# Third block of an attention and expert kernel: the chunk that two experts share is multiplied by their gates, turned to rows

## The chip, the cores and the metric

One core of a Trainium2 chip runs the whole program in one launch. The metric is the device time of one execution in microseconds; three executions of the kernel before are shown, and one further execution was profiled.

## The reference, cut to what matters

The input is x, 32 images of 128 tokens by 144 channels in f32, with one condition vector per image. Three transformer blocks follow each other, with a learned rotation between the first and the second. The change touches only the second half of the third block, a mixture of four experts:

```python
logits = h @ w_gate                       # 4 experts, the top 2 are kept
gate   = softmax over the kept two        # 0 for the others
for e in range(4):
    hidden = gelu(h @ w1[e] + b1[e])      # 144 -> 576
    y     += gate[:, e] * (hidden @ w2[e] + b2[e])   # 576 -> 144
x = x + g_mlp * y
```

All four experts are computed for every token, and the gate is zero for the two that are not kept.

## The kernel before, in words

The work is done in groups of G = 4 images, 8 groups a block. The order of the instructions is written out by hand: the main loop (L1281) runs over ticks, one image of attention each, and each tick has named gaps ("a", "e", "t", "stats", "b0", "b", "den", "pre1", "c", "y1", "y2", "z", "d" in the third block's order). `put(tick, gap, f, ...)` files a piece of other work under a gap, and `put2` files two halves of it in two gaps. Each engine executes its instructions in the order in which they were recorded, and waits for what they need.

An expert has 576 hidden units: four chunks of 128 and a rest of 64. Two experts make a pair, and the two rests share one chunk, number SHARED = 8 of `hid`, the first expert's in partitions 0 to 63 and the second's in 64 to 127. So a pair has NPC = 9 chunks of hidden units. `hid` is [128 units, 9 chunks, 4 images, 128 tokens].

- `moe1` (L1055) calls `fc1` (L930): three chunks at a time, weights as the stationary side, 4 x 128 tokens as the moving side, then GELU by ScalarE into `hid` (L947).
- `moe2` (L1059) calls `fc2` (L949) for one expert and one image: five products of 128x144 accumulate in one PSUM bank `ps_f`. A chunk of `hid` is the stationary side, w2 the moving side. The fifth product uses the shared chunk. Both experts of a pair multiply the same shared chunk, each with a copy of w2 in which the other's 64 rows are zero, so w2 has 10 chunks for 9 chunks of hidden units. VectorE then does acc = ps_f x gate + acc (L1064), with the gate as one number per token, which is a partition here.
- `moe_bias` (L1041) has GpSimd start `acc` with the four gated biases (L1051, L1053). `moe_out` (L1066) multiplies by g_mlp, adds to x and stores (L1069 to L1071).

For a group with first tick t0, the pair's tick is t0 + 8 or t0 + 10. There `moe1` stands in "stats"/"b0" and "den"/"pre1", and `moe2` of the first (even) expert and image 0 in "d". In the next tick come the third part of `moe1` and the even expert's images 1 to 3 ("b", "c", "d"). The second (odd) expert's images follow in gaps "a", "a", "b", "b" of the tick after that. The attention in the same ticks runs through `scores` (L819: ps_s, ps_w, the reduce nm at L854, the exponentials at L861), `weigh` (L867), `sums` (L885), `divide_T` (L897, transposes at L901), `largest_T` (L805, transpose at L808), `divide` (oT, L906), `largest` (q2, L813) and `project_out` (L922). In the pair's tick there is also other work of later groups: `values` (vaug, L802 and L803) beside the first pair, `qk_chunks` and `qk_masked` (the key masks, L727) beside the second.

PSUM has one bank for `ps_o` and seven that `bank` (L78) hands out; a bank comes free when its last reader is done. Every matrix product in f32 leaves two MATMUL records in the profile, a transpose leaves one.

Of the kernel before, what the change touches and what calls it, by code (L numbers as in the profile page):

```python
# [8 lines left out]
F32 = mybir.dt.float32  # L9
# [3 lines left out]
ALU = mybir.AluOpType  # L13
# [4 lines left out]
B, T, C = 32, 128, 144  # L18
# [4 lines left out]
NFC = 5  # L23


SHARED = 8
NPC = 9
MLP_COLS = NFC * (128 + 128 + C)
PAIR_COLS = NPC * 256 + 2 * NFC * C
D = 64  # L30
E = 4
G = 4
# [33 lines left out]
def tile_kernel(ctx: ExitStack, tc: tile.TileContext, a: dict, out: bass.AP):  # L66
    nc = tc.nc
# [10 lines left out]
    def bank(shape, name):  # L78

        n = 1  # L80
        for s in shape[1:]:
            n *= s
        t = ps_m.tile([128, 512], F32, tag="m", name=name)
        v = t[: shape[0], :n]
        if len(shape) == 3:
            v = v.rearrange("p (a b) -> p a b", b=shape[2])
        elif len(shape) == 4:
            v = v.rearrange("p (a b c) -> p a b c", b=shape[2], c=shape[3])
        return v
# [3 lines left out]
    ident = cst[:, K_ID : K_ID + 128]  # L93
# [16 lines left out]
    hid = const.tile([128, NPC, G, T], F32, name="hid")  # L110
# [49 lines left out]
    def views(t, n1, n2):  # L160

        p = Block()
        p.w1, p.w1R = t[:, : n1 * 128], t[:, n1 * 128 : n1 * 256]
        p.w2 = t[:, n1 * 256 : n1 * 256 + n2 * C].rearrange("p (m c) -> p m c", c=C)
        return p
# [452 lines left out]
    gr = defaultdict(dict)  # L618
# [311 lines left out]
    def fc1(g, p, name, m, to, rest_first):  # L930


        hM, hR = gr[g]["hM_m"], gr[g]["hR_m"]
        pss = [bank([128, G, T], f"ps_h_{name}_{m + i}") for i in range(len(to))]
        cols = [slice(128 * (m + i), 128 * (m + i) + 128) for i in range(len(to))]
        tiles = [rows4((m + i) % 3) for i in range(len(to))]
        yield from both(
            [(ps, p.w1[:, c], hM) for ps, c in zip(pss, cols)],
            [(ps, p.w1R[r, c], hR[r]) for ps, c, r in zip(pss, cols, tiles)],
            rest_first,  # L940
        )

        t = small.tile([128, 1], F32, tag="gelu", name=f"gelu_{name}_{m}", bufs=1)
        nc.scalar.activation(t, half, AF.Gelu_apprx_tanh)
        for ps, i in zip(pss, to):
            n = 64 if g[0] < 2 and i == SHARED else 128
            nc.scalar.activation(hid[:n, i], ps[:n], AF.Gelu_apprx_tanh)  # L947

    def fc2(g, w2, i, first, name):  # L949
        ps = bank([128, C], f"ps_f_{name}")  # L950
        for m in range(NFC):
            at0 = first + m if m < NFC - 1 else SHARED
            nc.tensor.matmul(ps, hid[:, at0, i, :], w2[:, m, :], start=m == 0, stop=m == NFC - 1)  # L953
        return ps
# [100 lines left out]
    def moe1(g, pair, part, rest_first):  # L1055
        to = ((0, 1, 2), (SHARED, 3, 4), (5, 6, 7))[part]
        return fc1(g, PAIRS[pair], f"3_{g[1]}_{pair}", 3 * part, to, rest_first)

    def moe2(g, e, i):  # L1059
        acc = gr[g]["acc"][:, i, :]  # L1060
        w2 = PAIRS[e // 2].w2[:, NFC * (e % 2) : NFC * (e % 2) + NFC, :]
        ps = fc2(g, w2, i, 4 * (e % 2), f"3_{g[1]}_{e}_{i}")
        w = gr[g]["cw"][:, i, e : e + 1]
        nc.vector.scalar_tensor_tensor(acc, ps, w, acc, ALU.mult, ALU.add)  # L1064

    def moe_out(g):  # L1066
        acc, n = gr[g]["acc"], g[1]
# [5 lines left out]
    late = L3 = None  # L1073
    PAIRS = []

    def load_pair(n, t):
        nc.sync.dma_start(t, a[f"L3_{n}_mlp"])
        PAIRS.append(views(t, NPC, 2 * NFC))

    def load_late():  # L1080
        nonlocal late, L3
# [6 lines left out]
        for k in ("wgate", "wgateR"):  # L1088
            setattr(L3, k, load(late, f"L3_{k}", q))
        load_pair(0, late.tile([128, PAIR_COLS], F32, name="pair0"))  # L1090

# [74 lines left out]
    stats = defaultdict(list)  # L1166

    def put(tick, gap, f, *args):
        gaps[tick, gap].append((f, args))

    def put2(tick, gap, to, f, *args):

        halves = []

        def first_half():
            halves.append(f(*args))
            next(halves[0])

        def second_half():
            for _ in halves[0]:  # L1180
                pass

        put(tick, gap, first_half)
        put(tick, to, second_half)

    for layer in range(3):
        ahead = 5 if layer == 0 else 6
        for n in range(NG):
            g = (layer, n)
            t0 = first[layer] + n * G  # L1190
            for i in range(G):
                s = layer * B + n * G + i
                if layer == 1 and i == 0:
                    put(t0 - ahead - 2, "d", rotate_T, n)
                    put(t0 - ahead - 1, "b", rotate_in, n)
                    put(t0 - ahead - 1, "d", rotate, n)
                stats[t0 + i - ahead].append((s, "a"))
                stats[t0 + i + 3].insert(0, (s, "m"))
                if layer < 2:
                    put(t0 + i - ahead + 1, "b", ln_T, s, "a")  # L1200
                else:
                    put(t0 + i - ahead, "d", ln_T, s, "a")
                if layer == 0:
                    put(t0 + i + 4, "a", ln_T, s, "m")
                else:
                    put(t0 + i + 3, "d", ln_T, s, "m")
                if layer == 0:
                    put(t0 + i - 3, "c", qk0_project, s)
                    put(t0 + i - 3, "z", qk0_variance, s)
                    put(t0 + i - 2, "b", qk0_guess, s)  # L1210
                    if s == 0:
                        for gap in "bbc":
                            put(-2, gap, qk0_newton, s, nc.vector)
                    else:
                        put(t0 + i - 2, "b", qk0_newton, s)
                        put(t0 + i - 1, "t", qk0_newton, s)
                        put(t0 + i - 1, "t", qk0_newton, s)
                    put(t0 + i - 1, "b", qk0_divide, s)
                    put(t0 + i - 1, "c", qk0_T, s)
            if layer == 0:  # L1220
                for i in (0, 2):
                    put(t0 + i // 2, "b", lambda g=g, i=i: list(values(g, i, 2)))
            elif layer == 1:
                put2(t0, "stats", "b", values, g, 0, 2, True)
                put2(t0 + 1, "stats", "b", values, g, 2, 2, True)
            else:
                put2(t0, "c", "c", values, g, 0, 2, True)
                put2(t0 + 1, "den", "pre1", values, g, 2, 2)
            if layer:
                put2(t0 - 2, "c", "c", qk_chunks, g)  # L1230
                put(t0 - 2, "z", qk_masked, g)
            if layer == 0:
                put2(t0 + 10, "stats", "b", mlp1, g, 0, (0, 1, 2), True)
                put2(t0 + 11, "d", "d", mlp1, g, 3, (3, SHARED), False)
                for i in range(G):
                    put(t0 + 12 + i // 2, "bd"[i % 2], mlp2, g, i)
            elif layer == 1:
                put2(t0 + 8, "c", "c", mlp1, g, 0, (0, 1, 2), True)
                put2(t0 + 9, "c", "c", mlp1, g, 3, (3, SHARED), True)
                for i in range(G):  # L1240
                    put(t0 + (10, 10, 11, 11)[i], "bdbc"[i], mlp2, g, i)
            else:
                put2(t0 + 7, "den", "pre1", gate_logits, g)
                put(t0 + 8, "e", expert_ranks, g)
                put(t0 + 8, "stats", expert_weights, g)
                for i in range(G):
                    put(t0 + 8 + i // 2, "cdab"[i], moe_bias, g, i)
                for pair in range(2):
                    at_ = t0 + 8 + 2 * pair
                    put2(at_, "stats", "b0", moe1, g, pair, 0, True)  # L1250
                    put2(at_, "den", "pre1", moe1, g, pair, 1, False)
                    put2(at_ + 1, "stats", "b0", moe1, g, pair, 2, True)
                    put(at_, "d", moe2, g, 2 * pair, 0)
                    put(at_ + 1, "b", moe2, g, 2 * pair, 1)
                    put(at_ + 1, "c", moe2, g, 2 * pair, 2)
                    put(at_ + 1, "d", moe2, g, 2 * pair, 3)
                    for i in range(G):
                        put(at_ + 2, "aabb"[i], moe2, g, 2 * pair + 1, i)
                put(t0 + 12, "b", moe_out, g)
# [4 lines left out]

    put(first[1] + B - 10, "c", load_L3)
    put(first[1] + B + 7, "d", lambda: load_pair(1, mlps[:, :PAIR_COLS]))

    def fill(tick, gap):
# [224 lines left out]
```

## Time and profile before

| what | value |
|---|---|
| three executions | 1420.84, 1423.7, 1427.12 us (median 1423.7) |
| the profiled execution | 1412.95 us |
| its span | 1411.1 us, granted clock 0.99 |
| third block's expert products, L953 | 1280 records, 16 x 2 x 4 images x 5 products |
| gated sums, L1064 on VectorE | 128, 46.9 us busy, 367 ns each |
| bias sums, L1051 and L1053 on GpSimd | 128 and 96, 386 to 390 and 488 ns each |
| out store, L1071 | 8 of 288 KB |
| a pair's weights | two loads of 1872 KB by SyncE's queue |

In the page, PE is the matrix engine and PEld its weight loads, DVE is VectorE, ACT is ScalarE, POOL is GpSimd and SP is SyncE. A row names line, engine, operation, what was written from what, the shapes, and the count. Busy time and the mean of one follow, and then the idle time of the engine just before such instructions and what ended it. The chain of waits goes back from the last instruction to whatever released each step. The timeline lists start, duration and instruction, and merges equal neighbours (x10). A matmul's row has its full duration, and the next one may start before it ends.

### The profile page before, as it was taken

What the parts mean: (1) busy time and instruction counts of PE and PEld (TensorE: products, weight loads), DVE (VectorE), ACT (ScalarE), POOL (GpSimd) and SP (SyncE); (2) the same over time, 40 slices, a digit from 0 to 9 for tenths busy, and PEclk for the clock granted to TensorE, in tenths of its full rate; (3) what the DMA queues carried; (4) which work ended last, traced back from release to release, by engine and by line L of the source; (5) the groups of instructions that cost most, each with busy time, mean ns of one, the idle gap of its engine ahead of it and who ended that gap; (6) DMA issues with size and microseconds to landing.
All of it is one profiled execution on the core that took longest, in us unless ns stands there. A gap on an engine that the chain in (4) does not pass through costs nothing.

```text
span 1411.1 us, 36544 instructions
## 1 busy us (share of the span) xinstructions
PE 1333.3 (94%) x14530; PEld 976.5 (69%) x14530; DVE 798.3 (57%) x2652; ACT 819.2 (58%) x1912; POOL 623.4 (44%) x1647
## 2 busy tenths in 40 slices
PE   6989898999989988999999999999999999999998
PEld 4667576686766566677767666777776767677765
DVE  5798888877864256565555555544444444343211
ACT  3657767656756445666666666555555555554431
POOL 5567667654643433343333334425252525151522
PEclk9999999999999999999999999999999999999999
DMA  8200000000003100000100000200000000000000
GB/s 221 57 2 19 19 19 2 19 3 20 19 1 117 34 2 18 10 19 10 42 27 18 10 18 11 73 10 18 9 19 9 19 10 18 10 18 2 18 9 9
DMA packets 21612, 34.78 MB, mean 25 GB/s; under 512 B 2176, under 2 KB 12256, under 8 KB 21184
## 3 DMA queue, kind: packets, MB, share of 16 engines
q1 hardware_dynamic: 20848, 31.82, 7.7%
q8 instruction: 117, 1.92, 0.6%
q10 hardware_dynamic: 592, 0.59, 0.2%
q14 instruction: 55, 0.45, 0.1%
HBM read 29.93 MB, written 2.47 MB: 23 GB/s over the span
## 4 chain that ended last, share of the span: by engine, by line
PE 68%; DVE 4%; ACT 2%; issue 1%; POOL 1%; POOLq 0%; DVEq 0%
PE ps_h L673 17%; PE ps_f L953 16%; PE ps_s L849 6%; PE ps_w L849 6%; PE ps_qk L673 5%; PE ps_o L876 5%; PE ps_pj L927 3%; PE ps_v L673 2%; PE ps_o L889 1%; DVE nm L854 1%; PE ps_o L901 1%; PE ps_g L673 1%; DVE oT L906 1%; PE ps_z L985 1%; PE ps_o L808 0%
## 5 line engine op out<-in xcount | busy, mean ns | idle before, releaser
L861 ACT ACTIVATE pr<-ps_w 128x512 f32<-128x512 f32 x384 | 208.5, 596 | 165.4 <-PE ps_w L849 164.7
L854 DVE TENSOR_REDUCE nm<-ps_s 128x4 f32<-128x512 f32 x384 | 246.8, 684 | 82.3 <-PE ps_w L849 68.9
L849 PE MATMUL ps_w<-q,kT 32*128 32x128 f32 x3072 | 236.4, 284 | 0.9 <-ACT hR_m L663 0.6
L849 PE MATMUL ps_s<-kT,qT 32*128 32x256 f32 x1536 | 234.8, 408 | 0.1
L849 PEld LDWEIGHTS ps_w<-q,kT 32*128 32x128 f32 x3072 | 198.6, 187 | 16.1 <-issue 3.6
L947 ACT ACTIVATE hid<-ps_h 128x512 f32<-128x512 f32 (+1 forms) x224 | 119.2, 590 | 119.1 <-PE ps_h L673 119.1
L953 PE MATMUL ps_f<-mlps,hid 128*128 128x144 f32 x1280 | 181.2, 292 | 0.5 <-ACT hid L947 0.5
L953 PEld LDWEIGHTS ps_f<-mlps,hid 128*128 128x128 f32 x1280 | 165.1, 191 | 18.4 <-issue 11.6
L913 POOL TENSOR_TENSOR x_sb<-x_sb,res_a 128x144 f32<-128x144 f32 x96 | 47.0, 489 | 266.8 <-DVE res_a L916 266.7
L1064 DVE SCALAR_TENSOR_TENSOR acc<-ps_f,cw,acc 128x144 f32<-128x144 f32 x128 | 46.9, 367 | 197.6 <-PE ps_f L953 175.8
L849 PEld LDWEIGHTS ps_s<-kT,qT 32*128 32x128 f32 x1536 | 135.0, 186 | 26.8 <-issue 9.2
L673 PE MATMUL ps_h<-hM_m,mlps 128*128 128x512 f32 x304 | 143.8, 606 | 0.0
L876 PE MATMUL ps_o<-pr,vaug 128*32 128x128 f32 x3072 | 104.8, 277 | 0.4 <-issue 0.4
L876 PEld LDWEIGHTS ps_o<-pr,vaug 128*32 128x32 f32 x3072 | 78.7, 110 | 33.8 <-PE ps_w L849 19.0
L673 PEld LDWEIGHTS ps_h<-hM_m,mlps 128*128 128x128 f32 x304 | 53.4, 190 | 66.2 <-issue 64.7
L906 DVE TENSOR_TENSOR oT<-on,ps_o 128x256 f32<-128x256 f32 x96 | 40.0, 417 | 96.3 <-PE ps_o L808 92.9
L953 PEld LDWEIGHTS ps_f<-pair,hid 128*128 128x128 f32 x640 | 82.3, 190 | 9.6 <-issue 8.4
L953 PE MATMUL ps_f<-pair,hid 128*128 128x144 f32 x640 | 86.8, 287 | 0.2 <-ACT hid L947 0.2
L913 POOL TENSOR_TENSOR x_sb<-x_sb,res_m 128x144 f32<-128x144 f32 x64 | 32.8, 512 | 111.4 <-DVE res_m L916 111.2
L634 POOL TENSOR_SCALAR rs_m_a<-mv_m_a 128x2 f32<-128x2 f32 x81 | 15.5, 191 | 142.9 <-DVE mv_m_a L632 115.5
L663 ACT ACTIVATE hM_m<-ps_hT_m,modM 128x128 f32<-128x128 f32 x96 | 44.1, 460 | 58.4 <-PE ps_hT_m L661 58.2
L861 ACT ACT_TABLE_LOAD x55 | 70.6, 1283 | 8.4 <-PE ps_w L849 7.6
(312 smaller groups left out, 2823.2 us busy)
## 6 DMA issues: line engine op xcount, KB each, us to landing
gates<-gates SPq DMA_DIRECT2D x48, 288.0 KB, 3.6
x_sb<-in_x SPq DMA_DIRECT2D x8, 288.0 KB, 10.2
out_x<-x_sb SPq DMA_DIRECT2D x8, 288.0 KB, 2.4
mlps<-in_L_mlp SPq DMA_DIRECT2D x2, 1000.0 KB, 6.3
wt<-in_W SPq DMA_DIRECT2D x6, 320.0 KB, 8.0
pair<-in_L_mlp SPq DMA_DIRECT2D x1, 1872.0 KB, 10.1
mlps<-in_L_mlp SPq DMA_DIRECT2D x1, 1872.0 KB, 7.6
mlps<-in_L_wmod SPq DMA_DIRECT2D x4, 290.0 KB, 6.3
```

The source lines that it names most:

```text
L663: nc.scalar.activation(gr[g][f"{k}_{kind}"][:, i, :], ps[:, k == "hR", :], AF.Identity, bias=m[:, sh, b : b + 1], scale=m[:, sc, b : b + 1],)
L673: nc.tensor.matmul(ps, x, y, start=k == 0, stop=k == 1)
L849: nc.tensor.matmul(o, x, y, start=True, stop=True)
L854: nc.vector.tensor_reduce(nmv[:, at0 : at0 + 2, ONE : ONE + 2], view.rearrange("p (r t k) -> p r t k", t=2, k=T), AX.X, ALU.max, negate=True,)
L861: nc.scalar.activation(pr[:, 4 * e : 4 * e + 4, :].rearrange("p s q -> p (s q)"), view, AF.Exp, scale=SCALE,)
L876: nc.tensor.matmul(po[rows4(j), t, :], v[:, 4 * j + 2 * t + r, :], prs[j // 2][:, 4 * (j % 2) + 2 * r + t, :], start=r == 0, stop=r == 1,)
L906: nc.vector.tensor_tensor(oT, st[s].pop("on"), po, ALU.mult)
L913: nc.gpsimd.tensor_tensor(x_sb[:, b, :], x_sb[:, b, :], t, ALU.add)
L927: nc.tensor.matmul(ps, oT[:, t, :], w[:, t, :], start=t == 0, stop=t == 1)
L947: nc.scalar.activation(hid[:n, i], ps[:n], AF.Gelu_apprx_tanh)
L953: nc.tensor.matmul(ps, hid[:, at0, i, :], w2[:, m, :], start=m == 0, stop=m == NFC - 1)
L1064: nc.vector.scalar_tensor_tensor(acc, ps, w, acc, ALU.mult, ALU.add)
```

## The change

The shared chunk is multiplied by the gates before it enters the product, so that one product with both experts' real w2 rows gives the two gated contributions at once.

The gates of a token lie in one partition, the tokens of `hid` along the free axis. So the gates are spread over 128 columns by GpSimd, 64 for each expert (`cwx`), turned by four transposes on PE, one an image, into a PSUM bank `ps_cw`, and multiplied into `hid[:, SHARED]` by VectorE. For this `shared_by_gate` is filed in the pair's tick, the copy in "stats" and the rest in "y1", ahead of `largest_T`, `divide` and the even expert's image 0 in "d".

`moe2` does four products for each expert. For the even expert it does a fifth, of the gated shared chunk, into a second half of the same bank, and VectorE adds that half to acc with a second instruction. The odd expert has no fifth product. w2 has 9 chunks a pair in place of 10, with no zero rows; the loads shrink accordingly.

```diff
-PAIR_COLS = NPC * 256 + 2 * NFC * C
+PAIR_COLS = NPC * (256 + C)
...
+    def shared_by_gate(g, pair):
+        cwx = late.tile([128, G, 2, 64], F32, tag="cwx", name=f"cwx_{g[1]}_{pair}", bufs=1)
+        cw = gr[g]["cw"][:, :, 2 * pair : 2 * pair + 2]
+        nc.gpsimd.tensor_copy(cwx, cw.unsqueeze(3).to_broadcast([128, G, 2, 64]))
+        yield
+        ps = bank([128, G, T], f"ps_cw_{g[1]}_{pair}")
+        for i in range(G):
+            nc.tensor.transpose(ps[:, i, :], cwx[:, i, :, :].rearrange("p e c -> p (e c)"), ident)
+        nc.vector.tensor_tensor(hid[:, SHARED], hid[:, SHARED], ps, ALU.mult)
+
     def moe2(g, e, i):
-        acc = gr[g]["acc"][:, i, :]
-        w2 = PAIRS[e // 2].w2[:, NFC * (e % 2) : NFC * (e % 2) + NFC, :]
-        ps = fc2(g, w2, i, 4 * (e % 2), f"3_{g[1]}_{e}_{i}")
+        acc, w2, at0 = gr[g]["acc"][:, i, :], PAIRS[e // 2].w2, 4 * (e % 2)
+        ps = bank([128, 2, C], f"ps_f_3_{g[1]}_{e}_{i}")
+        for m in range(4):
+            nc.tensor.matmul(
+                ps[:, 0, :], hid[:, at0 + m, i, :], w2[:, at0 + m, :], start=m == 0, stop=m == 3
+            )
+        if e % 2 == 0:
+            nc.tensor.matmul(
+                ps[:, 1, :], hid[:, SHARED, i, :], w2[:, SHARED, :], start=True, stop=True
+            )
         w = gr[g]["cw"][:, i, e : e + 1]
-        nc.vector.scalar_tensor_tensor(acc, ps, w, acc, ALU.mult, ALU.add)
+        nc.vector.scalar_tensor_tensor(acc, ps[:, 0, :], w, acc, ALU.mult, ALU.add)
+        if e % 2 == 0:
+            nc.vector.tensor_tensor(acc, acc, ps[:, 1, :], ALU.add)
...
                     put2(at_ + 1, "stats", "b0", moe1, g, pair, 2, True)
+                    put2(at_, "stats", "y1", shared_by_gate, g, pair)
                     put(at_, "d", moe2, g, 2 * pair, 0)
...
-        none = np.zeros((64, C), w1.dtype)
-        w2 = np.vstack([w2[0], none, w2[1][:512], none, w2[1][512:]])
+        w2 = np.vstack([w2[0][:512], w2[1][:512], w2[0][512:], w2[1][512:]])
```

In the changed kernel the copy is at L1064, the transposes at L1068, the multiplication at L1069, the products at L1077 and (the shared chunk) L1081, the gated sum at L1085, the addition at L1087, and `moe_out` at L1092 to L1094.

More of the change, by code (lines that the diff above doesn't have):

```diff
@@ L1077, in load_pair @@
         nc.sync.dma_start(t, a[f"L3_{n}_mlp"])
-        PAIRS.append(views(t, NPC, 2 * NFC))
+        PAIRS.append(views(t, NPC, NPC))
     def load_late():
```

## The prediction

> **What bounds the kernel now.** I read the page first (busy shares and the chain that ended last), then the chain in one stretch of the third block, then each engine in order of time around the edited step, and last the rows that give a duration to each operation. The edit lies in the third block's expert part, from about 902 us to the end. The page's head and its chain:
>
> ```profile
> span 1411.1 us, 36544 instructions
> ...
> PE 1333.3 (94%) x14530; PEld 976.5 (69%) x14530; DVE 798.3 (57%) x2652; ACT 819.2 (58%) x1912; POOL 623.4 (44%) x1647
> ```
> ```profile
> PE 68%; DVE 4%; ACT 2%; issue 1%; POOL 1%; POOLq 0%; DVEq 0%
> ```
>
> The chain is PE's. Over 905 to 1300 us the table by stage has PE busy for 394.0 of 395 us, DVE for 168.4 and POOL for 152.2, at a granted clock of 1.00. Busy PE is not PE at its peak, so the pitch of the products decides. The chain through a step of group 2 (start, length, what):
>
> ```profile
> 1049.49 0.22 PE ps_o L901 x2
> 1049.71 0.11 PE ps_o L808
> 1049.82 1.23 PE ps_f L953 x10
> 1051.05 0.11 PE ps_hT_m L660
> 1051.16 0.11 PE ps_hT_m L661
> ```
>
> No gap is left between pieces. Five expert products leave ten records and take 1.23 us, so one 128x144 product costs 0.245 us. A transpose leaves one record and takes 0.11 us.
>
> **Removed.** For each of 8 groups and 2 pairs, 4 images lose one product (the odd expert's fifth). That is 16 x 4 = 64 products, 64 x 0.245 = 15.7 us of PE. They lie in the unbroken chain, four at a time in gaps "a" and "b" of the tick after next, between other PE work, so they count in full.
>
> **Added on PE.** 16 x 4 = 64 transposes of 128x128. Here a rule speaks against the change. The row:
>
> ```profile
> L901 PE MATMUL ps_o<-cst,rdx x192: 272/273/421, 70.0 to 1330.3; 128*128 128x128 f32 x192
> ```
>
> One transpose lasts 273 ns. The Trainium skill (TensorE: Matmul & The Clock Gate, Part 4: PE-mode transpose) puts a 128x128 transpose in a kernel at about 275 ns, most of it access latency, and adds that its result lies in PSUM and needs a further step. At that price 64 x 0.275 = 17.6 us is more than the 15.7 saved, and the change loses 1.9 us. But 273 ns is a latency: in the chain the next instruction follows 0.11 us later. So PE pays 4 x 0.11 = 0.44 us a pair, 7.0 us for 16. I take the pitch, since four transposes stand together and nothing in front of them is late.
>
> Not all 16 pairs pay. In the last three (group 6's second pair and both of group 7) attention is over, and PE stands at the chunk whose GELU is late:
>
> ```profile
> 1344.86 1.00 PE L953 MATMUL ps_f<-mlps,hid 128*128 128x144 f32 x6
> 1344.96 1.57 ACT L947 ACTIVATE hid<-ps_h 128x512 f32<-128x512 f32 x3 [5.39 <-PE ps_h L673]
> 1346.09 0.76 PE L953 MATMUL ps_f<-mlps,hid 128*128 128x144 f32 x4 [0.23 <-ACT hid L947]
> ```
>
> Six records at 0.1225 are issued by 1345.60 and the seventh starts at 1346.09: a hole of 0.49 us, which takes the 0.44. In group 5's second pair the chain has 1.28 us of nm on DVE ahead of L808, which hides it too. Twelve pairs pay: 12 x 0.44 = 5.3 us. If those covers were gone, 1.8 us more.
>
> **Added on DVE, and the new wait.** The product hid x gates is a TENSOR_TENSOR of 128x512 with one side in PSUM. The same form stands in the exponential's part:
>
> ```profile
> L564 DVE TENSOR_TENSOR hid<-hid,ps_even x2: 678/682/687, 192.8 to 199.5; 128x512 f32<-128x512 f32 x2
> ```
>
> So 16 x 0.68 = 10.9 us, and 64 additions into acc at about 0.31 (the row of L916, 128x144 from PSUM) are 19.6 us: 30.5 us on an engine with over 200 us free. Time on DVE is free; lateness is not. The fifth product of the even expert's image 0 must now wait for DVE, and behind it on PE stand two to four transposes, the projection and the next scores. DVE in that step of group 2:
>
> ```profile
> 1049.72 0.23 DVE L803 COPY vaug<-ps_v 128x72 f32<-128x72 f32 x1
> 1049.86 0.42 DVE L906 TENSOR_TENSOR oT<-on,ps_o 128x256 f32<-128x256 f32 x1
> 1050.20 0.41 DVE L813 TENSOR_TENSOR q<-qT,ps_o 128x256 f32<-128x256 f32 x1
> 1051.16 0.37 DVE L1064 SCALAR_TENSOR_TENSOR acc<-ps_f,cw,acc 128x144 f32<-128x144 f32 x1 [0.55 <-PE ps_hT_m L660]
> ```
>
> With the timeline's starts (L808 at 1049.55, first product at 1049.66), the gate transposes take L808's place at 1049.55. The last starts at 1049.88 and ends at 1050.15. DVE starts 0.04 later (as oT does after L808), is free since 1049.95, and ends at 1050.87; PE can go at 1050.92. PE meanwhile does L808 (1049.99) and four products from 1050.10, and reaches the fifth at 1051.08. The wait is hidden with 0.16 us to spare, or 0.04 if its weight load, about 0.12 ahead, has to wait too. Bounds: 0, or about 0.1 us in the eleven pairs of this kind; I allow 0.2 us in all.
>
> What moves on DVE: oT and q end about 1.0 us later (1051.29 and 1051.63), against the projection at 1051.32 + 0.44 = 1051.76 and the next w scores at 1051.92 + 0.44 = 1052.36. Both are in time. In the second pair's step the key masks follow:
>
> ```profile
> 948.03 1.41 DVE L727 TENSOR_SCALAR kT<-ps_qk,cst 128x512 f32<-128x512 f32 x2 [0.45 <-ACT kT L721]
> ```
>
> There the second mask ends at 949.44 now and a bank of ps_w waits for it (start 949.50). In that step the gates' product runs 947.17 to 947.84, oT and q to 948.5, the masks from 948.43 to 949.84. The bank is ready 0.4 us later, PE arrives 0.44 later: no new stall, no gain. The additions delay the next DVE entries (rd, oT, res_a) by 0.31 us; rd has 0.4 us of idle ahead of it in the plain tick of group 0 (920.70 to 921.10), the others stand behind PE work of over 0.5 us. PSUM takes one more bank a pair: its releaser is a GELU or a reduce that is done before PE gets there in each step I followed.
>
> **Added on POOL.** 16 copies of the gates, 128x512. No row has this form. With one input, 191 ns for 2 elements (L634) and 385 for 144 (L1051) give 0.9 us at 512; with two inputs, 488 for 144 and 1400 for 576 give 1.27. I take 0.9, the nearer kind. POOL in the first pair's step:
>
> ```profile
> 1041.65 0.39 POOL L643 TENSOR_SCALAR xr<-x_sb,rs_m_a 128x64 f32<-128x64 f32 x1
> 1043.77 1.40 POOL L1069 TENSOR_TENSOR acc<-acc,gates 128x576 f32<-128x576 f32 x1 [1.73 <-DVE acc L1064]
> ```
>
> The gates are ready at 1039.75, the copy falls into the 1.73 us hole, and PE asks for it near 1049. Without that hole the first bias sum (ends 1049.85, wanted by DVE at 1051.16) still has 1.3 us. Cost 0. No DMA is added or moved on a queue; a pair's load shrinks from 3744 to 3600 columns, outside the chain.
>
> **Sum.** -15.7 + 5.3 + 0.2 = -10.2 us. The profiled execution took 1412.95 us (span 1411.1), so 1402.8. The median of the shown runs, 1423.7, is 10.8 above that execution, and the three spread over 6.3 us; the saving is taken off the median: 1413.5.
>
> **The rivals.**
> - *The main case* (chance 0.69): the sum holds within about 2 us, 1411.5 to 1416.
> - *DVE is late* (0.19): the slack of 0.16 us is too small and every steady tick loses some 0.4 us at the fifth product or at a bank that the masks or additions release. 12 x 0.4 = 4.8, so -5.4: 1418.3. For it: the slack is one semaphore long, and DVE gains 30 us. Against it: in the last pairs PE resumed 0.05 us after the GELU ended.
> - *The won time is given back* (0.06): PE gets earlier to waits on POOL's bias sums or ACT's exponentials, and the 64 products buy nothing but pay for the transposes: near 0, 1423. Against it: no piece of the chain over 1034 to 1054 is ACT's or POOL's.
> - *Slower* (0.06): the round trip lies bare. If PE stops at the first even product instead of the fifth, each steady pair pays the transposes at latency (0.33 + 0.27 = 0.60), the handoffs (0.09) and DVE (0.68), or 1.4 us, and with transposes unpipelined 1.9. At 1.9: 12 x 1.9 = 22.8 - 15.7 = +7.1, 1430.8. It decides from 15.7 / 12 = 1.31 us of PE a pair. Against it: PE waited for single chunks of hid at 1346.09, not for the whole tile, and in the changed order the wait stands on the fifth product.
>
> Half a per cent, 7.1 us, is about what can be told from no change. The main case is faster by more than that except at its edge: faster 0.69, same 0.25 (the two middle rivals), slower 0.06. The range runs from the sum with the runs' spread, 1409, to the DVE case with it, 1421.
>
> **What would show it.** Expert products fall from 1280 to 1152 records in the third block (1920 to 1792 in all). The L1068 transposes start 0.11 us apart; the product L1069 takes 0.68 us; ps_f at L1081 shows no idle ended by hid L1069; the copy L1064 takes about 0.9 us and L1092 still waits for DVE. From 1345 on the stretch shrinks by over 0.9 us a pair. An idle of over 0.3 us at L1081, or a copy over 3 us, makes the prediction wrong.

## The result and the profile after

Ten runs of the changed kernel have a median of 1406.82 us (1398.87 to 1413.49). Ten runs of the kernel before on the same chip have 1420.7 (1410.26 to 1427.12). The ratio, estimated over all these runs, is 0.9912, with a 95% interval of 0.9884 to 0.9939: 12.5 us less, with an interval from 8.7 to 16.5 (the two medians lie 13.9 us apart). The predicted ratio was 1413.5 / 1423.7 = 0.9928, inside that interval. The predicted level, 1413.5 with a range from 1409 to 1421, is not met.

The profiled execution took 1403.12 us, against a forecast of 1402.8 for it. Its page begins, and its chain adds up, as follows:

```profile
span 1401.4 us, 36513 instructions
...
PE 1329.2 (95%) x14466; PEld 973.3 (69%) x14466; DVE 827.4 (59%) x2732; ACT 820.8 (59%) x1912; POOL 633.2 (45%) x1663
...
PE 68%; DVE 3%; ACT 2%; issue 1%; POOL 1%; POOLq 0%; DVEq 0%
```

PE has 64 records fewer (128 product records gone, 64 transposes come), VectorE is busy for 29.1 us more and GpSimd for 9.8 us more, and the chain is still PE's in the same share. The chain through the same step of group 2 as before (start, length, what):

```profile
1047.29 0.22 PE ps_o L901 x2
1047.51 0.44 PE ps_cw L1068 x4
1047.94 0.11 PE ps_o L808
1048.05 0.98 PE ps_f L1077 x8
1049.04 0.27 PE ps_f L1081 x2
1049.31 0.11 PE ps_hT_m L660
```

The four transposes cost 0.44 us in the chain, as their pitch said (the pitch is the distance from one start to the next). The fifth product costs 0.27 us where a product costs 0.245: at most 0.03 us of waiting. The even expert's five products of image 0 take 1.25 us in each of the first eleven pairs, where the kernel before has 1.23, so this wait is 0.3 us in all. The groups of the new instructions (busy us, mean ns of one, idle time before them and what ended it):

```profile
L1087 DVE TENSOR_TENSOR acc<-acc,ps_f 128x144 f32<-128x144 f32 x64 | 19.4, 304 | 2.2
L1081 PE MATMUL ps_f<-pair,hid 128*128 128x144 f32 x64 | 13.4, 290 | 0.0
L1081 PE MATMUL ps_f<-mlps,hid 128*128 128x144 f32 x64 | 13.3, 289 | 0.0
L1092 POOL TENSOR_TENSOR acc<-acc,gates 128x576 f32<-128x576 f32 x8 | 11.2, 1402 | 32.3 <-DVE acc L1085 32.3
L1069 DVE TENSOR_TENSOR hid<-hid,ps_cw 128x512 f32<-128x512 f32 x16 | 11.0, 688 | 37.4 <-PE ps_o L808 23.4 <-ACT hid L947 11.8 <-PE ps_cw L1068 2.1
L1064 POOL COPY cwx<-cw 128x512 f32<-128x512 f32 x16 | 9.8, 612 | 21.8 <-DVE cw L1038 21.8
L1068 PE MATMUL ps_cw<-cst,cwx 128*128 128x128 f32 x64 | 9.8, 275 | 0.0
```

No idle time at L1081 is put down to VectorE, and the eight final multiplications on GpSimd (L1092) still wait for VectorE, as forecast. VectorE around the same step, and below it the fifth product and its weight load (start, length):

```profile
1048.05 0.69 DVE L1069 TENSOR_TENSOR hid<-hid,ps_cw 128x512 f32<-128x512 f32 x1 [0.32 <-PE ps_o L808]
1048.65 0.41 DVE L906 TENSOR_TENSOR oT<-on,ps_o 128x256 f32<-128x256 f32 x1
1048.99 0.41 DVE L813 TENSOR_TENSOR q<-qT,ps_o 128x256 f32<-128x256 f32 x1
1049.41 0.37 DVE L1085 SCALAR_TENSOR_TENSOR acc<-ps_f,cw,acc 128x144 f32<-128x144 f32 x1
...
1047.34 0.60 PE L1068 MATMUL ps_cw<-cst,cwx 128*128 128x128 f32 x4
1048.79 0.30 PEld L1081 LDWEIGHTS ps_f<-pair,hid 128*128 128x128 f32 x2
1048.87 0.43 PE L1081 MATMUL ps_f<-pair,hid 128*128 128x144 f32 x2
```

The multiplication ends at 1048.74, and in the timeline the fifth product starts at 1048.87. Its weight load starts at 1048.79, 0.05 us behind the end of the multiplication. So the round trip is covered but for those 0.03 us, with nothing left over.

**A measure that the spread of runs doesn't reach.** Two profiles of the changed kernel agree within 0.02 us at every image of the third block, while the two executions differ by 2.1 us (1403.12 and 1405.22). Only where TensorE's clock is halved for a few microseconds does the block take longer. So below, "the third block" is the time from the first product of the projection of image 69 (898.08 us before, 897.73 after; the first transposes of gates come some 13 us later) to the end of the span: 513.04 us before and 503.67 after, a difference of -9.37 us against the -10.2 of the sum.

### The profile page after: what moved, and what is told of

The parts are those of the page before. It is cut to its first block, busy times and chain, and to the rows that moved or that the text cites. A ratio compares the mean times of both kernels' runs of the same rounds, so it can differ in the third digit from the quotient of the medians.

```text
span 1401.4 us, 36513 instructions
## 1 busy us (share of the span) xinstructions
PE 1329.2 (95%) x14466; PEld 973.3 (69%) x14466; DVE 827.4 (59%) x2732; ACT 820.8 (59%) x1912; POOL 633.2 (45%) x1663
## 4 chain that ended last, share of the span: by engine, by line
PE 68%; DVE 3%; ACT 2%; issue 1%; POOL 1%; POOLq 0%; DVEq 0%
PE ps_h L673 18%; PE ps_f L1077 9%; PE ps_s L849 6%; PE ps_w L849 6%; PE ps_qk L673 5%; PE ps_o L876 5%; PE ps_f L953 5%; PE ps_pj L927 3%; PE ps_v L673 2%; PE ps_o L889 1%; PE ps_f L1081 1%; DVE nm L854 1%; PE ps_o L901 1%; PE ps_g L673 1%; DVE oT L906 1%
## 5 line engine op out<-in xcount | busy, mean ns | idle before, releaser
L1085 DVE SCALAR_TENSOR_TENSOR acc<-ps_f,cw,acc 128x144 f32<-128x144 f32 x128 | 46.8, 367 | 156.0 <-PE ps_f L1081 74.9
L953 PE MATMUL ps_f<-mlps,hid 128*128 128x144 f32 x640 | 93.3, 293 | 0.0
L953 PEld LDWEIGHTS ps_f<-mlps,hid 128*128 128x128 f32 x640 | 81.9, 190 | 8.1 <-issue 3.3
L1077 PEld LDWEIGHTS ps_f<-pair,hid 128*128 128x128 f32 x512 | 66.8, 190 | 8.4 <-issue 7.7
## 6 DMA issues: line engine op xcount, KB each, us to landing
x_sb<-in_x SPq DMA_DIRECT2D x8, 288.0 KB, 10.2
```

The source lines that it names most:

```text
L1077: nc.tensor.matmul(ps[:, 0, :], hid[:, at0 + m, i, :], w2[:, at0 + m, :], start=m == 0, stop=m == 3)
L1085: nc.vector.scalar_tensor_tensor(acc, ps[:, 0, :], w, acc, ALU.mult, ALU.add)
```

## The experiments

Theory P is the prediction's: PE's pitch decides, so that 64 products are gained and the transposes paid by pitch. All medians and ratios below stand beside runs of the kernel before on the same chip, whose medians were 1418.7 to 1419.3 us in 38 to 64 runs. A difference in us beside a ratio is worked out from the ratio.

### The changed kernel again

> The changed kernel once more, to separate the size of the saving from the spread of runs. Theory P (PE's issue pitch: 64 products at 0.245 us gained, 12 times four transposes at 0.11 us paid): 10.2 us below the kernel before, ratio 0.9928, in whichever place the runs of this chip lie. Rival S (there is a further saving that the sum left out): 12.5 us or more below again, ratio 0.991 or less. If the spread of runs comes from the half-speed stretches of TensorE's clock, the time of a run goes with its granted clock, about 1 us for every 0.1% of clock.

Measured: 1406.72 us (1401.36 to 1417.24), ratio 0.9923 (0.9899 to 0.9948), or 10.9 us less than 1419.3. The third block is 503.68 us, 0.01 us from the first profile. Over the ten runs of the first measurement the time goes with the granted clock: 1413.5 at 0.976 and 0.977, 1398.9 to 1403.2 in four of the five from 0.989 up (1410.2 in the other). But the clock is not all of it: of the 38 runs of the kernel before in the last set, five have a granted clock of 0.987 and range from 1414.6 to 1427.7. What follows: the saving of the sum, 10.2 us, lies in both intervals. The runs do not exclude rival S's 12.5, but the third block shows no more than 9.4.

### Only the removal

```diff
-        ps = fc2(g, w2, i, 4 * (e % 2), f"3_{g[1]}_{e}_{i}")
+        ps, at0 = bank([128, C], f"ps_f_3_{g[1]}_{e}_{i}"), 4 * (e % 2)
+        to = (0, 1, 2, 3, SHARED)[: 5 - e % 2]
+        for m, j in enumerate(to):
+            j = j if j == SHARED else at0 + j
+            nc.tensor.matmul(
+                ps, hid[:, j, i, :], w2[:, m, :], start=m == 0, stop=m == len(to) - 1
+            )
```

> Kernel before, with only the odd expert's fifth product taken out and nothing put in its place; it leaves out the odd expert's share of the 64 rest units. Theory P: 64 x 0.245 = 15.7 us below the kernel before. Rival G (the won time is given back at waits for POOL, ACT or DVE): 8 us or less. Rival S (products are worth more than their pitch): 18 us or more.

Measured: 1399.75 us, ratio 0.9879 (0.9851 to 0.9907), 17.2 us less. The third block is 497.40 us, -15.64. Each pair gains 0.98 us, four products at 0.245, from the first to the last. The removal is worth what the pitch said, and nothing of it is given back.

### Only the turning of the gates

In the changed kernel's `moe2`:

```diff
-        for m in range(4):
-            nc.tensor.matmul(
-                ps[:, 0, :], hid[:, at0 + m, i, :], w2[:, at0 + m, :], start=m == 0, stop=m == 3
-            )
-        if e % 2 == 0:
-            nc.tensor.matmul(
-                ps[:, 1, :], hid[:, SHARED, i, :], w2[:, SHARED, :], start=True, stop=True
-            )
+        for m, j in enumerate((at0, at0 + 1, at0 + 2, at0 + 3, SHARED)):
+            nc.tensor.matmul(
+                ps[:, 0, :], hid[:, j, i, :], w2[:, j, :], start=m == 0, stop=m == 4
+            )
...
-        if e % 2 == 0:
-            nc.vector.tensor_tensor(acc, acc, ps[:, 1, :], ALU.add)
```

> Only the gates' turning is added: copy, four transposes and the multiplication as in the change, but both experts keep their fifth product, in the same accumulation as in the kernel before, and VectorE has no second addition. The shared chunk is thus gated twice. Theory P: 12 x 0.44 = 5.3 us above the kernel before, or up to 5.5 with the wait. Rival L (a transpose costs its 0.275 us): 13 to 17.6 us above. Rival D (VectorE is late for the fifth product): 10 us above.

Measured: 1421.42 us, ratio 1.0036 (1.0012 to 1.0061), 5.1 us more. The third block is 518.14 us, +5.11. Up to image 91 there are eleven pairs and +4.87 us, 0.44 each. The five pairs behind them pay 0.24 together. So the turning costs its pitch (with the 0.03 us of waiting a pair in it), and the last pairs hide the rest, as the prediction had it for four of these five (the late GELU in the last three, nm in group 5's second).

### The transposes twice

```diff
-        for i in range(G):
+        for i in 2 * list(range(G)):
             nc.tensor.transpose(ps[:, i, :], cwx[:, i, :, :].rearrange("p e c -> p (e c)"), ident)
```

> The changed kernel, with the four transposes of a pair done twice into the same bank. Theory P: 12 x 0.44 = 5.3 us above the changed kernel of the same call; up to 7 us where the cover of the last pairs is used up. Rival L (latency): 13 to 17.6 us above it. Rival H (the transposes lie in a hole of PE that is there anyway): 0 to 2 us above it.

Measured: 1415.75 us, ratio 0.9981 (0.996 to 1.0003), 8.2 us above the changed kernel by the two ratios. The third block is 510.05 us, 6.38 above it: 4.8 in the first eleven pairs and 1.6 in the last five. The pitch holds; 64 times the latency of 273 ns would have made 17.5 us. In the last five pairs, eight transposes find less cover than four: of the second four's 2.2 us they hide only 0.6.

### The shared product first

```diff
+        if e % 2 == 0:
+            nc.tensor.matmul(
+                ps[:, 1, :], hid[:, SHARED, i, :], w2[:, SHARED, :], start=True, stop=True
+            )
         for m in range(4):
...
-        if e % 2 == 0:
-            nc.tensor.matmul(
-                ps[:, 1, :], hid[:, SHARED, i, :], w2[:, SHARED, :], start=True, stop=True
-            )
```

> The changed kernel with one change of order: for the even expert the product of the gated shared chunk is issued ahead of the other four in place of behind them. Theory P: the four products (0.98 us) are what hides VectorE's multiplication; in the changed kernel's trace at group 2 the multiplication ends at 1048.74 and the fifth product starts at 1048.87, so put first (1047.89) it would stand about 0.9 us in each of the 12 steady pairs: 11 us above the changed kernel, near the kernel before. Rival N (the wait is already bare, or PE has other slack behind it): 0 to 2 us above.

Measured: 1421.73 us, ratio 1.0029 (1.0011 to 1.0048). The third block is 516.42 us, 12.7 above the changed kernel and 3.4 above the kernel before. PE in the timeline of group 2:

```profile
1047.62 0.27 PE L808 MATMUL ps_o<-cst,nm 128*128 128x128 f32 x1
1048.63 0.51 PE L1077 MATMUL ps_f<-pair,hid 128*128 128x144 f32 x2 [0.74 <-DVE hid L1069]
```

L1077 is the shared product here. The next start after L808 would be 0.11 us later; it is 1.01 us, so PE stands for 0.9 us. This is the prediction's slower rival, made real: the place of one product among five decides whether the third block gains 9 us or loses 3.

### The multiplication twice

```diff
         nc.vector.tensor_tensor(hid[:, SHARED], hid[:, SHARED], ps, ALU.mult)
+        nc.vector.tensor_tensor(hid[:, SHARED], hid[:, SHARED], ps, ALU.mult)
```

> The changed kernel with VectorE's multiplication of the shared chunk done twice, so that the chunk carries the squared gates; it measures the slack ahead of the fifth product. Theory P: 0.69 us more on a path with 0.13 us of slack: PE stands 0.5 to 0.6 us at L1081 in 12 pairs, 6 to 7 us above the changed kernel. Rival N (VectorE is not on any path here): 0.

Measured: 1423.42 us, ratio 1.0026 (1.0006 to 1.0046). The third block is 515.93 us, 12.3 above the changed kernel, twice what was expected. The fifth product (L1082 in this file) among the groups, and in the timeline of group 2's step:

```profile
L1082 PE MATMUL ps_f<-pair,hid 128*128 128x144 f32 x64 | 13.9, 300 | 3.9 <-DVE hid L1070 3.9
L1082 PE MATMUL ps_f<-mlps,hid 128*128 128x144 f32 x64 | 13.9, 299 | 3.4 <-DVE hid L1070 3.4
...
1061.22 1.15 PE L1078 MATMUL ps_f<-pair,hid 128*128 128x144 f32 x8
1062.85 0.51 PE L1082 MATMUL ps_f<-pair,hid 128*128 128x144 f32 x2 [0.48 <-DVE hid L1070]
1063.20 0.27 PE L660 MATMUL ps_hT_m<-cst,xh_m 128*128 128x128 f32 x1
```

Idle time of 7.3 us is put down to the second multiplication. In group 2's step the five products take 1.98 us, 0.73 more than in the changed kernel, all of the 0.69 and a little: the slack of 0.13 us that I read from the start of the product was not there, since the weight load, which reads the gated chunk, must wait too. The same growth stands in each of the first eleven pairs, 8.0 of the 12.3 us. Another 1.1 lies in the steps after the second pairs of groups, and 3.2 in the last five pairs; what makes these was not traced.

### Transposes in gap c

```diff
-                    put2(at_, "stats", "y1", shared_by_gate, g, pair)
+                    put2(at_, "stats", "c", shared_by_gate, g, pair)
```

> The changed kernel with the four transposes and the multiplication filed in gap c in place of y1, so that for the first pair of a group the transposes stand ahead of the values' products, where PE waits some 0.4 us for a bank that a GELU releases. Theory V (the hole takes the transposes): six pairs no longer pay 0.44 us, up to 2.6 us below the changed kernel. Rival B (the transposes' own bank moves the wait on to the next bank, and the hole returns behind them): no difference, or up to 2 us above.

Measured: 1410.63 us, ratio 0.9934 (0.9912 to 0.9956). The third block is 503.48 us, 0.2 below the changed kernel. In the step of a first pair, the weight loads of the values' products in the changed kernel, and then PE's timeline and ScalarE's GELUs in this kernel:

```profile
1045.60 0.29 PEld L673 LDWEIGHTS ps_v<-rotU,hR_a 32*128 32x128 f32 x2
1046.09 0.29 PEld L673 LDWEIGHTS ps_v<-rotU,hR_a 32*128 32x128 f32 x2 [0.20 <-ACT hid L947]
...
1053.90 0.66 PE L1068 MATMUL ps_cw<-cst,cwx 128*128 128x128 f32 x4
1054.49 0.76 PE L673 MATMUL ps_v<-rotU,hR_a 32*128 32x144 f32 x4
1053.11 1.57 ACT L947 ACTIVATE hid<-ps_h 128x512 f32<-128x512 f32 x3 [5.11 <-PE ps_h L673]
```

In the changed kernel the hole is 0.2 us, and not the 0.4 that was expected, so six pairs could win some 1.2 us and not 2.6. In this kernel the values' products run without it. But the transposes start 0.1 us late, and the products follow them after 0.59 us where their pitch is 0.44. Together this is the old hole again, and no pair gains more than 0.1 us. The outcome is rival B's, "no difference". Its reason, a wait for the next bank that a GELU frees, is not shown: the second of the three GELUs ends near 1054.20, and the products start 0.29 us later.

### The additions behind res_a

In `moe2`, for image 0 of the even expert, the vector part goes to gap a of the next tick:

```diff
+        if e % 2 == 0 and i == 0:
+            yield
         w = gr[g]["cw"][:, i, e : e + 1]
...
-                    put(at_, "d", moe2, g, 2 * pair, 0)
+                    put2(at_, "d", "a", moe2, g, 2 * pair, 0, later=1)
```

> The changed kernel with image 0's two gated additions recorded behind the projection's res_a instead of ahead of it; PE's order is unchanged. In the changed kernel's trace the second addition (0.30 us) moves res_a from 949.21 to 949.56, res_a frees a PSUM bank, and the third ps_h chunk and all behind it come 0.15 us later, in the step after each second pair (0.3 in the last such). Theory A (this addition is what the added VectorE work costs): 5 x 0.15 + 0.3, or about 1 us below the changed kernel. Rival M (the reduce nm stands next and is now late by as much): no difference, or worse.

The reading behind it: the changed kernel's VectorE in the step after group 0's second pair, and PE's third ps_h product there,

```profile
946.37 0.69 DVE L1069 TENSOR_TENSOR hid<-hid,ps_cw 128x512 f32<-128x512 f32 x1 [4.31 <-PE ps_o L808]
946.97 0.41 DVE L906 TENSOR_TENSOR oT<-on,ps_o 128x256 f32<-128x256 f32 x1
947.30 0.41 DVE L813 TENSOR_TENSOR q<-qT,ps_o 128x256 f32<-128x256 f32 x1
947.63 1.40 DVE L727 TENSOR_SCALAR kT<-ps_qk,cst 128x512 f32<-128x512 f32 x2
948.95 0.36 DVE L1085 SCALAR_TENSOR_TENSOR acc<-ps_f,cw,acc 128x144 f32<-128x144 f32 x1
949.34 0.30 DVE L1087 TENSOR_TENSOR acc<-acc,ps_f 128x144 f32<-128x144 f32 x1
949.56 0.30 DVE L916 TENSOR_TENSOR res_a<-ps_pj,gates 128x144 f32<-128x144 f32 x1
949.92 0.69 PE L673 MATMUL ps_h<-hR_m,mlps 32*128 32x512 f32 x1
```

against the kernel with only the turning, which has no second addition and whose trace runs 0.01 to 0.02 us ahead there:

```profile
948.93 0.36 DVE L1081 SCALAR_TENSOR_TENSOR acc<-ps_f,cw,acc 128x144 f32<-128x144 f32 x1
949.21 0.30 DVE L916 TENSOR_TENSOR res_a<-ps_pj,gates 128x144 f32<-128x144 f32 x1
949.85 0.59 PE L673 MATMUL ps_h<-hR_m,mlps 32*128 32x512 f32 x1
```

res_a ends at 949.86 instead of 949.51, the third ps_h product starts at 949.92 instead of 949.85, and the weighted sums behind it (ps_o) at 950.97 instead of 950.80.

Measured: 1409.97 us, ratio 0.9937 (0.9916 to 0.9958). The third block is 506.36 us. A half-clock stretch lies in this execution at 1106.4, and the two images around it take 1.67 us more than the same two of the next groups; without that it is 1.0 above the changed kernel. The order doesn't help: the step after each second pair takes as long as in the changed kernel, and the step after each first pair takes 0.1 to 0.2 us more, which makes the 1.0. VectorE in the same step:

```profile
959.09 0.29 DVE L916 TENSOR_TENSOR res_a<-ps_pj,gates 128x144 f32<-128x144 f32 x1
959.30 0.35 DVE L1087 SCALAR_TENSOR_TENSOR acc<-ps_f,cw,acc 128x144 f32<-128x144 f32 x1
959.69 0.30 DVE L1089 TENSOR_TENSOR acc<-acc,ps_f 128x144 f32<-128x144 f32 x1
```

Now the addition is last, at 959.99, and the same ps_h product starts at 960.05, again 0.06 us behind. Whichever of the two banks is freed last, PE waits for the end of the same sum of work. The repair failed: it is this sum of work that costs, and not which instruction comes first.

### Without the second addition

```diff
-        if e % 2 == 0:
-            nc.vector.tensor_tensor(acc, acc, ps[:, 1, :], ALU.add)
```

> The changed kernel without VectorE's second addition; it leaves out the shared chunk's contribution, which PE still computes. Theory A: the 0.10 to 0.15 us after each second pair (0.3 in the last such) are gone, 0.7 to 1 us below the changed kernel. Rival N (VectorE's additions are free): 0. Rival D (VectorE bounds the expert part now): 10 us or more below.

Measured: 1408.44 us, ratio 0.9919 (0.9881 to 0.9957), which does not tell 1 us. The third block does: 502.51 us, 1.16 below the changed kernel. Of this, 0.15 us lies in the step after each second pair of the first four groups, 0.34 in that of the fifth, and 0.23 from image 94 on. And -15.64 + 5.11 = -10.53 is exactly this kernel's difference from the kernel before.

### The shared product with the odd expert

```diff
-        if e % 2 == 0:
+        if e % 2 == 1:
             nc.tensor.matmul(
                 ps[:, 1, :], hid[:, SHARED, i, :], w2[:, SHARED, :], start=True, stop=True
             )
...
-        if e % 2 == 0:
+        if e % 2 == 1:
             nc.vector.tensor_tensor(acc, acc, ps[:, 1, :], ALU.add)
```

> The changed kernel with the shared product and its addition moved from the even expert's step to the odd expert's, two ticks after the multiplication. Theory A (what the change paid beyond removal and transposes, about 1.2 us in the third block, is the second addition that keeps a PSUM bank from PE in the step after each second pair, plus the weight load of the fifth product waiting for VectorE): both are gone, about 1 us below the changed kernel from the first pair on, 10.4 us below the kernel before; up to 0.4 us of it may be lost at the very end, where the last addition comes later. Rival M (the additions are only late in another place): no difference. In medians the 1 us is near what the runs can tell; the profiles tell it.

Measured: 1412.11 us, ratio 0.9954 (0.9934 to 0.9975). The third block is 507.45 us; less 1.67 for a half-clock stretch at 1102.1, it is 2.1 above the changed kernel. A group gains 0.64 us on the kernel before where the changed kernel gains 0.93, which makes 1.4 us in five groups. The stretch from image 91 on is 1.7 us longer, but 1.0 of it are four products that this kernel does behind that mark and the changed kernel ahead of it; 0.7 is left. PE in the step of group 0's second pair, and VectorE and ScalarE just ahead:

```profile
954.42 0.37 PE L849 MATMUL ps_s<-kT,qT 32*128 32x256 f32 x1
954.79 0.38 PE L849 MATMUL ps_w<-q,kT 32*128 32x128 f32 x2
953.26 1.40 DVE L727 TENSOR_SCALAR kT<-ps_qk,cst 128x512 f32<-128x512 f32 x2
954.28 0.46 ACT L663 ACTIVATE hR_a<-ps_hT_a,modR 128x128 f32<-128x128 f32 x1
```

The next ps_w products come 0.37 us after the ps_s product. The second key mask on VectorE (L727) is done at 954.66, but they start 0.05 us behind ScalarE's hR_a, which ends at 954.74, and the trace has their weight load wait for ScalarE. In the third block such waits for hR_a come four times, 1.6 us in all, and the changed kernel has none. The 1.4 us of the groups agree with these waits. Why PE waits for this instruction only in this order, and where the 0.7 us at the end go, was not traced. Theory A's repair falls a second time, and the cost is above the "no difference" of rival M.

### The same, with the multiplication twice

> As the kernel with the shared product in the odd expert's step, with VectorE's multiplication done twice (squared gates on the shared chunk). Where the fifth product stood close behind it, the second multiplication cost 0.73 us a pair, 12.3 us in the third block's profile. Theory A: two ticks later nothing waits for it; what is left is oT and q 0.69 us later on VectorE, 0 to 0.3 us a pair, 0 to 4 us in all. Rival Q (oT and q were what cost it): still about 0.7 us a pair, 11 us.

Measured: 1419.95 us, ratio 1.0004 (0.9977 to 1.0031). The third block is 511.71 us, 5.9 above the kernel that it is derived from (with the 1.67 taken off that one). This is more than the 4 expected and half of rival Q's 11. So the second multiplication also costs where no product stands close behind it: something that VectorE does after it (oT, q, the masks) must come late to PE. Which of the three costs the 5.9 was not separated. Nor is it a share of the 12.3 us with the even expert: there the fifth product's step alone grew by 8.0 us in eleven pairs, and one stop of PE can cover both delays.

## Why the prediction was right and wrong

**The step that failed** is the last of the sum: "the saving is taken off the median: 1413.5", and with it the low end of the range, "the sum with the runs' spread, 1409". The measured median, 1406.82, is 6.7 us below 1413.5. Of these, 3.0 us are the level: the median of the three runs, 1423.7, was no good one. Ten runs gave 1420.7, and later sets of 38 to 64 gave 1418.7 to 1419.3. The other 3.7 us are what the two medians of ten differ by (13.9) beyond the sum (10.2). The third block shows no such further saving, and the second set had 10.9 by its ratio, so the runs' spread is the likely reason, but no run separates it. The low end had to hold the uncertainty of the level, for which three runs spread over 6.3 us, as well as the spread of the runs after (1398.87 to 1413.49); it stood only 4.5 us under 1413.5.

The mechanism was right, and its sum nearly so. The profiled execution's sum, 1402.8, came out at 1403.12, but that closeness is partly luck: the two executions have their half-clock stretches in different places. Free of these, the difference is -9.4 us. That the predicted ratio lies inside the measured interval is luck in part as well, since the interval is 8 us wide.

**Removed, -15.7:** -15.64 measured alone. Right.

**Transposes, 12 x 0.44 = +5.3:** +5.11 measured alone, eleven pairs at 0.44 and 0.24 in the other five; the wait of the next term is in it. Right, and the choice of the pitch over the latency decided the sign: at the 0.275 us that the prediction weighed, paid by all 64, the sum would have been a loss.

**The wait at the fifth product, +0.2 allowed:** 0.03 us in each of eleven pairs, 0.3 in all. The prediction's second reading (the weight load has to wait too) was the true one, as the doubled multiplication showed. But its 0.04 us of slack was not there: VectorE starts 0.11 us after the last transpose ends (1047.94 to 1048.05), where the prediction had 0.04.

**The additions, at nothing:** wrong in size. The prediction said that res_a, delayed by 0.31, stood "behind PE work of over 0.5 us". In the step after each second pair VectorE has no idle time from the gates' multiplication to res_a, and PE waits there for a bank that the last of them frees. Without the additions the third block is 1.16 us shorter, 0.93 of it in these steps, and with the removal and the turning the sum is -15.64 + 5.11 + 1.16 = -9.37, the measured difference. The check in this is that removal and turning, each measured alone, add up to the -10.53 of the kernel without the addition.

**The copy on GpSimd, about 0.9 us:** 0.612 us, and hidden. **The rival of the late VectorE** was seen in its place but at a quarter of its price (1.16 for 4.8). **The won time given back** falls with the removal alone. **The slower rival** is real, and is one line of order away: +3.4 us in the third block with the shared product first, between the 12 x 1.4 - 15.7 = +1.1 and the +7.1 that the prediction gave it.

## What to carry to other kernels

In a chain of PE work without gaps, an instruction costs the distance to the next start and not its duration, and what hides a round trip through another engine is the work issued between: count to the weight load that needs the result, not to the product. An engine with 40% idle time still costs where it runs without a pause and PE waits for a bank behind it, and reordering work inside such a stretch moves the wait without shortening it. Put a saving on a level only if that level has enough runs; otherwise widen the range by what the level doesn't know.

## What was unexpected

The third block's stretches from one image to another repeat to 0.02 us between two profiles of the changed kernel, while the runs spread over 15 us. TensorE's clock explains a part: there are stretches of about 3.4 us, or of a multiple of it, at half clock. One of them stands just ahead of the third block's first mark in the kernel before and not in the changed one. The tables by stage of before and of after have the granted clock in the third column from the right (0.57 and 1.00):

```profile
894.00:898.00 4.00, 4.00 (x21) 3.81 (x19) 1.92 (x5) 1.09 (x3) 0.59 (x2) 0.57 0.30 52
```

```profile
894.00:898.00 4.00, 3.92 (x42) 3.26 (x38) 2.81 (x10) 1.62 (x4) 1.73 (x4) 1.00 0.23 47
```

The two that fell inside the third block, at 1102.1 and at 1106.4, cost 1.67 us each, in the middle of unbroken PE work (PE is busy for all of 1101 to 1111 in both, at a granted clock of 0.83). Most of the others lie in the first 520 us, many of them at nearly the same places from execution to execution: all thirteen traces have one that starts between 404 and 419. In the third block eleven of the thirteen have none before the last 10 us or so. No run here tells what starts them.
